# Reordering the score products and computing each token's values once in a banded-attention and mixture-of-experts kernel

## The chip, the cores and the metric

The kernel runs on one core of a Trainium2 chip. The metric is the device time of one execution in microseconds (us). Three executions of the kernel before the change took 786.92, 786.96 and 787.59 us; the median is 786.96 us. One more execution was recorded by the hardware profiler and gave the trace that all views below are read from.

## What is computed

Input x holds 16 sequences (batches) of 512 tokens with 128 features. Cut to what matters, the reference is:

```python
mod = (silu(c) @ wmod).reshape(16, 6, 1, 128)        # sa, ca, ga, sb, cb, gb per batch
h = layernorm(x) * (1 + ca) + sa
q, k, v = h @ wq.T + bq, h @ wk.T + bk, h @ wv.T + bv    # 16 heads of 8 features
scores = q k^T * 8**-0.5, only where |i - j| <= 32       # window of 32 tokens either way
x = x + ga * (softmax(scores) @ v) @ wo.T + bo ...
h = layernorm(x) * (1 + cb) + sb
gate = softmax(h @ gate_w.T); top 2 of 8 experts per token
x = x + gb * (sum of the 2 routed experts + one shared expert)   # silu(h@w1) * (h@w3) @ w2
```

## The kernel before, in words

**Tiles.** A batch is four blocks of 128 tokens. Attention works on one block at a time: a *step* is (batch b, block u), 64 steps in all. Because keys lie up to 32 tokens outside a block, `hT` (normalized input, features on partitions) and `kT` are padded by 32 zero columns on either side.

**One step** (the loop in lines 1026 to 1050) issues, in this order:

1. `weights` (line 424): score products into two PSUM tiles `t` of two banks each, with the negated row maximum added by a matmul; then `exp(0)` on ScalarE (line 444, `w<-t`) for the first tile.
2. `average` (line 449): for the step before, 64 small matmuls of `w` with `v_own`, the values; they go into spare columns of a score tile `s`. ScalarE copies the sums out as `raw` (line 464).
3. `transposed` (line 415): four matmuls `neg` turn the next step's row maxima, and ScalarE copies them as `sh` (line 421). Then `other_half`, which is `exp(1)`.
4. `between(b, u, 0)`: a place. A place runs closures from the table `places` (lines 950 to 969), then routing and scattering work.
5. `divided` (line 998): two transposes of `raw` (line 471), then `rec` and `o` on VectorE (lines 474 and 475), which end the softmax.
6. `between(b, u, 1)`, where most steps start a *gated product*: two products `uv` into a PSUM tile, tanh on ScalarE (`g`, line 554), two VectorE operations (`g` and `h`, lines 555 and 557). It is `uv_sh`, `g_sh`, `h_sh` (shared expert, batch b-2) in a batch's first step, and a group of routed rows in the other three once routed rows exist.
7. `look_ahead(n + 3)`: `row_max` (line 386) of the step three ahead: 4 band matmuls and 32 score matmuls into two PSUM tiles `s`, then two VectorE maxima `neg` (line 402), then GpSimd splits them into bf16 pieces (lines 408 to 412).
8. `between(b, u, 2)` and `between(b, u, 3)`: other transposes and products. In a batch's first step these are `oT` (line 497) and `ys` (line 535, the shared expert's last product, which reads `h_sh`); in the second `xT` and `xnT`; in the third `xT`, `h2T`, `q`, `lg`; in the fourth `xT` and `k`.

The order of all engines' instructions is this written order (`manual_schedule`); each engine runs its own list in order and waits for semaphores.

**Buffers that decide waits.** PSUM pool `ps_s` has three tiles of two banks (tag `s`), shared by `t`, `s` and the gated products. Pool `ps_m` has two one-bank tiles (tag `m`, function `misc`) that serve every transpose and every other product in turn, so each waits for the reader of the one two before it. `average` writes into the second `s` tile of the last `row_max`, taken from the list `spare`.

**Values.** `project_v` (line 358) computes a batch's values for eight overlapping windows of 128 keys, one every 64 tokens: 8 matmuls, in two halves of 4, each half in one PSUM tile followed by one ScalarE copy (line 369) into one of three `v_own` tiles. It runs in places (1, 0) and (3, 0) of the batch before. A `v_own` tile keeps a head's 8 values, a column of ones and zeros up to 32 columns.

Of the kernel before, what the change touches and what calls it, by code (L numbers as in the profile page):

```python
# [10 lines left out]
F32 = mybir.dt.float32  # L11
# [8 lines left out]
P = 128  # L20
B, S, D = 16, 512, 128
H, DH, WINDOW = 16, 8, 32
E = 8
NT = S // P
QB = 64
# [4 lines left out]
NU = S // U  # L30
G, J = 4, 4
SP = S + 2 * WINDOW
# [18 lines left out]
def adaln_block(ctx: ExitStack, tc: tile.TileContext, x, wq, bq, wk, bk, wv, bv, wo, bo,  # L51
# [3 lines left out]
    const = ctx.enter_context(tc.tile_pool(name="const", bufs=1))  # L55
# [5 lines left out]
    def mm(o, lhsT, rhs, start=True, stop=True):  # L61
        nc.tensor.matmul(o, lhsT, rhs, start=start, stop=stop)  # L62
# [81 lines left out]
    pieces_of = [const.tile([P, 4, G, 32], BF16, name=f"pieces{n}") for n in range(NPC)]  # L144


    NVO = 3
    v_own_of = [const.tile([P, 2, 4 * 8 * 32 + 16], F32, name=f"v_own{n}") for n in range(NVO)]
    smallT = const.tile([P, 27], F32, name="smallT")
    modT = const.tile([P, 6, B], F32, name="modT")  # L150
    wT = [const.tile([P, D], F32, name=f"wT{n}") for n in range(4)]
    wqT, wkT, wvT, woT = wT
# [22 lines left out]
    with ExitStack() as c1:  # L175
# [5 lines left out]
        def misc(name):  # L181
            return ps_m.tile([P, 512], F32, tag="m", name=name)
# [65 lines left out]
        def zero_but_ones(t):  # L248
            nc.gpsimd.memset(t, 0.0)
            nc.gpsimd.memset(  # L250
                t[:, :, 0 : 4 * 8 * 32].rearrange("p s (m c) -> p s m c", c=32)[:, :, :, DH : DH + 1], 1.0
            )

        def operands():
# [5 lines left out]
        def more_operands():  # L260
            for t in pieces_of[2:]:
                nc.gpsimd.tensor_copy(t.rearrange("p i g r -> p (i g r)"), pieces_0)
            zero_but_ones(v_own_of[2])
            nc.gpsimd.memset(zero, 0.0)

        def gate(t, shape, name):
# [90 lines left out]

        def project_v(b):

            m = made[b]  # L360
            hT = m.hT
            m.v_own = []
            for half in range(2):
                ps = misc(f"v_{b}_{half}")
                for n in range(4):
                    i = half * 4 + n
                    mm(ps[:, n * D : (n + 1) * D], hT[:, i * QB : i * QB + P], wvT)
                t = v_own_of[(2 * b + half) % NVO]
                nc.scalar.copy(
                    t[:, :, 0 : 4 * 8 * 32].rearrange("p s (m c) -> p m s c", c=32)[:, :, :, 0:DH],  # L370
                    ps.rearrange("p (m s c) -> p m s c", s=2, c=DH),
                )
                m.v_own += [(t.rearrange("p s c -> p (s c)"), 8 * n) for n in range(4)]
                yield

        def edge(u):
# [72 lines left out]
        def average(b, u, w, v_own):  # L449

            t = spare.pop() if spare else ps_s.tile([P, 2, 512], F32, tag="s", name=f"o_{b}_{u}")
            spare.clear()
            w = w.rearrange("p g (a h j q) -> p g a h j q", a=2, h=2, j=J)
            for a in range(2):
                c = slice(4 * KM + a * QB, 4 * KM + (a + 1) * QB)
                v, m0 = v_own[2 * u + a]
                for s in range(2):
                    for n in range(2):
                        for g in range(G):
                            k0 = s * 4 * 8 * 32 + (m0 + 2 * g + n) * 32  # L460
                            mm(t[32 * g : 32 * g + 32, n, c], v[:, k0 : k0 + 32], w[:, g, a, :, 2 * n + s, :],
                               start=s == 0, stop=s == 1)
            raw = wk_p.tile([P, 2, U], F32, tag="raw", name=f"raw_{b}_{u}", bufs=2)
            nc.scalar.copy(raw, t[:, :, 4 * KM : 4 * KM + U])
            return raw
# [445 lines left out]
        def routing():  # L911

            for g, r in list(routes.items()):
                if next(r, 0) is None and g < len(GROUPS):
                    return

        def scattering():
            if scatters and next(scatters[0], 0) is not None:
                scatters.pop(0)
                n_sorted[0] += 1  # L920

        raw_of = []
        AHEAD = 3
# [4 lines left out]
        def projecting(b):  # L928
            if b < B:
                if b not in projects:  # L930
                    projects[b] = project(b)
                    values[b] = project_v(b)
                next(projects[b], None)
# [42 lines left out]
        def between(b, u, n):  # L976
            for f in places.get((u, n), []):
                f(b)
            if n < 3 or b == B - 1:
                routing()  # L980
            if n == 0 and raw_of:
                window[:] = [None, raw_of[-1]]
                scattering()
                combining()
                window.clear()
            n_places[0] += 1
            fetch_some()

        def look_ahead(n):
            if n < len(steps):  # L990
                b, u = steps[n]
                maxima[b, u] = row_max(b, u, made[b].kT, made[b].q_own)
# [11 lines left out]
        with tc.manual_schedule():  # L1004
            nc.gpsimd.memset(neg_half, -0.5)
            projecting(0)
            before_first()
            operands()
            for _ in range(5):
                projecting(0)  # L1010
            look_ahead(0)
            projecting(1)
            projecting_v(0)
            projecting_v(0)
            look_ahead(1)
            projecting(1)
            more_operands()
            transposed(0)
            projecting(1)
            look_ahead(2)  # L1020
            projecting(1)
            once = before_second()
            copies = experts_and_zeros()
            spare.clear()
            pending = None
            for n, (b, u) in enumerate(steps):
                m = made[b]
                if u == 0:
                    m.o = act.tile([P, NT, D], F32, tag="o", name=f"o_{b}")
                w, other_half = weights(b, u, m.kT, m.q_own, maxima.pop((b, u)))  # L1030
                if pending is not None:
                    raw = average(*pending)
                    raw_of[:] = [raw]
                transposed(n + 1)
                other_half()
                between(b, u, 0)
                if pending is not None:
                    divided(pending, raw)
                if n == 0:
                    projecting(1)  # L1040
                between(b, u, 1)
                if n == 0:
                    projecting(1)
                look_ahead(n + AHEAD)
                between(b, u, 2)
                if n < 3:
                    next(once, None)
                next(copies, None)
                between(b, u, 3)
                pending = (b, u, w, m.v_own)  # L1050

            beat_c()
            beat_b()
            divided(pending, average(*pending))
            for n in range(2):
                load_every(n)
            units = [(b, e) for b in range(SORTED, B) for e in (E, *range(E))]
            t = ps_s.tile([P, 2, 512], F32, tag="s", name="sums")
            sums += [t[:, n, :] for n in range(2)]
            x_next = h_last = None  # L1060
            stores = []

            def tick():
                for b in range(B - 3, B):
                    finishing(b)
                routing()
                window[:] = [None, None]
                scattering()
                combining()
                window.clear()  # L1070
                n_places[0] += 2
                fetch_some()

            while units or x_next or h_last or stores or len(stream) > n_done[0] or combines:
                tick()
                beat_a()
                stores = [r for r in stores if next(r, 0) is None]
                x_now, x_next = x_next, None
                if units and units[0][0] in h2T_of and (units[0][1] == E or units[0][0] in scores_T):
                    x_next = (*units[0], scaled(*units.pop(0)))  # L1080
                beat_b()
                h_now = None
                if x_now:
                    b, e, xe = x_now
                    h_now = b, e, gated(f"all_{b}_{e}", lambda o, n: mm(o, matrices(e)[n], xe), 0, 1)
                tick()
                beat_c()
                if h_last:
                    added(*h_last)
                    if h_last[1] == E - 1:  # L1090
                        stores.append(stored(h_last[0]))
                h_last = h_now
            assert n_done[0] == len(stream) and not combines
# [81 lines left out]
```

## Time and profile before

| what | value |
|---|---|
| median of three executions | 786.96 us |
| profiled execution, its own time | 860.98 us |
| its span, first to last instruction | 859.2 us |
| mean granted TensorE clock | 0.931 |
| TensorE busy (page, part 1) | 80% of the span |
| VectorE, ScalarE, GpSimd busy | 52%, 49%, 50% |
| 64 steps: first `t` to the start of the last step | 30.2 to 674.9 us |
| the tail: routed rows of the last batches, two batches computed by all experts | 674.9 to 859.2 us |

A reader of the page takes part 1 (busy time by engine) first, then part 4 (the chain of work that ended last). The trace also gives groups of instructions by form (busy time, mean ns of one, idle time before them and what ended it), a list of waits (who waited for whom: total us, times, longest), and a timeline in which each row has the start, the length, the engine, the line, and what it writes and reads. In those, PE is TensorE, PEld its weight loads, DVE VectorE, ACT ScalarE, POOL GpSimd. The profiled execution is 74 us longer than the median of the others.

### The profile page before, as it was taken

The page shows a single profiled execution, that of the slowest core. Times are in us where ns is not written, and L with a number is a line of the kernel's source. Part 1 is how long each engine was busy: PE and PEld are TensorE (multiplying, and loading weights), DVE is VectorE, ACT ScalarE, POOL GpSimd, SP SyncE. Part 2 cuts the span into 40 slices and gives each one's busy share as a digit, 9 for nine tenths or more (in the row PEclk, how much of TensorE's full clock was granted, in tenths as well). Part 3 has the DMA queues.
Part 4 walks back from the last instruction along what each step waited for, and adds up shares of the span by engine and source line. Part 5 has one row for each costly group of instructions (what it writes and reads, how often), then busy time and mean ns, then how long its engine had stood idle before and what let it go on. Part 6 is the DMA issues. An engine that isn't in the chain of part 4 may idle for free.

```text
span 859.2 us, 26167 instructions
## 1 busy us (share of the span) xinstructions
PE 687.0 (80%) x10792; PEld 513.3 (60%) x10792; DVE 443.9 (52%) x1058; ACT 423.2 (49%) x733; POOL 426.0 (50%) x934
## 2 busy tenths in 40 slices
PE   5889999877898888987888897789868564866980
PEld 3557677655676766676766676566656453544630
DVE  2544656835358354445655254763637433654482
ACT  3657777555675554654555555546433421222310
POOL 3533333486522566526466564555553646334265
PEclk9999999999999998998899999999988777998896
DMA  5071301112332435361453345345314344666644
GB/s 168 3 217 40 92 7 39 41 33 69 102 105 74 122 98 161 87 171 29 134 176 106 115 119 158 100 130 150 113 54 137 111 150 125 199 200 202 185 108 109
DMA packets 119510, 97.49 MB, mean 113 GB/s; under 512 B 9125, under 2 KB 113487, under 8 KB 119391
## 3 DMA queue, kind: packets, MB, share of 16 engines
q1 hardware_dynamic: 91834, 70.70, 29.3%
q0 software_dynamic: 7168, 14.69, 5.7%
q10 hardware_dynamic: 20388, 10.43, 4.1%
q8 instruction: 84, 1.38, 0.7%
q14 instruction: 36, 0.29, 0.1%
HBM read 66.39 MB, written 30.97 MB: 113 GB/s over the span
## 4 chain that ended last, share of the span: by engine, by line
PE 48%; DVE 13%; issue 13%; ACT 10%; POOL 6%; another core or an unknown queue 5%; DMA 3%; SPq 2%; POOLq 0%; DVEq 0%; ACTq 0%
PE s L62 12%; PE t L62 9%; PE uv L62 5%; POOL yg L806 4%; DVE neg L402 3%; ACT w L444 2%; PE q L62 2%; PE uv_sh L62 2%; PE xT L211 2%; PE raw L471 2%; PE ys L62 2%; PE ye L62 2%; PE lg L62 2%; PE v L62 2%
## 5 line engine op out<-in xcount | busy, mean ns | idle before, releaser
L444 ACT ACTIVATE w<-t 128x1024 f32<-128x1024 f32 x128 | 131.6, 1028 | 70.3 <-PE t L62 62.9
L806 POOL DMA_INDIRECT yg<-result,r_posi x112 | 110.7, 989 | 92.8 <-DVE yg L819 45.4
L402 DVE TENSOR_REDUCE neg<-s 128x8 f32<-128x768 f32 x128 | 116.8, 953 | 55.2 <-PE s L62 21.9
L410 POOL CAST pieces<-neg 128x16 bf16<-128x16 f32 x192 | 56.2, 293 | 163.8 <-DVE neg L402 154.2
L724 POOL DMA_INDIRECT table<-rows,r_posi x112 | 112.1, 1001 | 26.2 <-issue 25.5
L62 PEld LDWEIGHTS s<-w,v_own 128*32 128x32 f32 x3904 | 64.0, 115 | 42.0 <-issue 27.1
L62 PE MATMUL s<-w,v_own 128*32 128x64 f32 x3904 | 78.5, 228 | 9.7 <-issue 9.4
L62 PE MATMUL uv<-xT,wg 128*128 128x128 f32 x608 | 82.1, 293 | 0.2 <-issue 0.2
L62 PEld LDWEIGHTS <-packed 32*128 32x128 bf16 (+2 forms) x1101 | 32.4, 95 | 83.0 <-issue 68.4
L62 PEld LDWEIGHTS uv<-xT,wg 128*128 128x128 f32 x608 | 77.8, 207 | 6.1 <-issue 5.7
L62 PE MATMUL t<-q_own,kT 32*128 32x256 f32 x1024 | 77.5, 411 | 0.0
L62 PE MATMUL s<-kT,q_own 32*128 32x96 f32 x2048 | 71.9, 274 | 3.0 <-issue 2.0
L474 DVE RECIPROCAL rec<-raw 128x16 f32<-128x16 f32 x64 | 16.2, 253 | 111.7 <-PE raw L471 111.7
L62 PEld LDWEIGHTS s<-kT,q_own 32*128 32x128 f32 x2048 | 70.9, 193 | 3.7 <-issue 3.6
L555 DVE SCALAR_TENSOR_TENSOR g<-g,uv 128x512 f32<-128x512 f32 x38 | 26.1, 687 | 73.2 <-issue 33.2
L62 PE MATMUL t<-packed 32*128 32x256 bf16 x512 | 35.1, 289 | 26.7 <-DVE neg L402 20.6
L62 PEld LDWEIGHTS t<-q_own,kT 32*128 32x128 f32 x1024 | 54.0, 205 | 2.8
L774 ACT COPY xT<-xT 128x512 f32<-128x512 f32 x38 | 22.2, 585 | 67.6 <-PE xT L211 43.2
L554 ACT ACTIVATE g<-uv 128x512 f32<-128x512 f32 x38 | 22.7, 598 | 62.2 <-PE uv L62 29.7
L211 PE MATMUL xT<-wide,xg 128*128 128x128 f32 x152 | 28.3, 302 | 27.5 <-DMA xg<-table 14.6
L195 POOL TENSOR_SCALAR veps_f<-mv_f 128x4 f32<-128x4 f32 x16 | 5.7, 356 | 77.0 <-DVE mv_f L191 77.0
L62 PE MATMUL ye<-wg,h 128*128 128x128 f32 x304 | 42.6, 284 | 0.2 <-DVE xe L843 0.2
(188 smaller groups left out, 1340.9 us busy)
## 6 DMA issues: line engine op xcount, KB each, us to landing
wg<-experts SPq DMA_DIRECT2D x152, 192.0 KB
xg<-table SPq DMA_DIRECT2D x38, 256.0 KB
result<-ye ACTq DMA_DIRECT2D x38, 256.0 KB
mb<-mod_rows SPq DMA_DIRECT2D x16, 320.0 KB
x<-in_L_attn_x_dram SPq DMA_DIRECT2D x16, 256.0 KB
table<-zero SPq DMA_DIRECT2D x8, 512.0 KB
out_dram<-x SPq DMA_DIRECT2D x16, 256.0 KB
xb<-out_dram SPq DMA_DIRECT2D x14, 256.0 KB
```

The lines of the kernel that those rows point to most:

```text
L62: nc.tensor.matmul(o, lhsT, rhs, start=start, stop=stop)
L211: nc.tensor.transpose(ps[:, t * P : (t + 1) * P], src[:, t, :], ident)
L402: nc.vector.tensor_reduce(neg[:, :, 2 * n : 2 * n + 2].rearrange("p i g -> p g i"), tiles[n][:, :, 0 : 4 * KM].rearrange("p g (i k) -> p g ...
L410: nc.gpsimd.tensor_copy(pieces[:, :, :, n], neg)
L444: nc.scalar.activation(w[:, 2 * n : 2 * n + 2, :], tiles[n], AF.Exp, scale=SCALE)
L471: nc.tensor.transpose(ps[:, n * P : (n + 1) * P], raw[:, n, :], ident)
L474: nc.vector.reciprocal(rec, both[:, :, DH])
L554: nc.scalar.activation(a, t[:, 0, :], AF.Tanh, scale=0.5)
L555: nc.vector.scalar_tensor_tensor(a, a, 1.0, t[:, 0, :], ALU.add, ALU.mult)
L724: stored = nc.gpsimd.indirect_dma_start(out=table[g % 2][:, :], out_offset=bass.IndirectOffsetOnAxis(ap=r.pos[:, k, n0 + t : n0 + t + 1], ...
L774: nc.scalar.copy(xT, ps)
L806: nc.gpsimd.indirect_dma_start(out=y[:, t, :], out_offset=None, in_=result[g][:, :], in_offset=bass.IndirectOffsetOnAxis(ap=r.pos[:, k, s ...
```

## The change

It makes two edits.

**Order within a step.** `look_ahead(n + 3)` moves from behind `between(b, u, 1)` to directly behind `between(b, u, 0)`, ahead of `divided`. So the `s` matmuls and the two `neg` maxima now come before the `raw` transposes, before `rec` and `o`, and before the step's gated product. (In the very first step two pieces of `project(1)` move along with it.)

```diff
                 between(b, u, 0)
+                if n == 0:
+                    projecting(1)
+                    projecting(1)
+                look_ahead(n + AHEAD)
                 if pending is not None:
                     divided(pending, raw)
-                if n == 0:
-                    projecting(1)
                 between(b, u, 1)
-                if n == 0:
-                    projecting(1)
-                look_ahead(n + AHEAD)
                 between(b, u, 2)
```

**Values once per token.** `project_v` computes the 576 padded tokens once, in 4 matmuls of 128 rows and one of 64, and copies them to two tiles, `even` (windows that begin at a multiple of 128) and `odd` (those that begin 64 later). The odd tile's halves come from different partitions, so there are six ScalarE copies instead of two. There are four `v_own` tiles, 48 columns for a pair of heads instead of 64.

```diff
-    NVO = 3
-    v_own_of = [const.tile([P, 2, 4 * 8 * 32 + 16], F32, name=f"v_own{n}") for n in range(NVO)]
+    PAIR = 48
+    v_own_of = [const.tile([P, 4 * 8 * PAIR], F32, name=f"v_own{n}") for n in range(4)]
...
-            for half in range(2):
-                ps = misc(f"v_{b}_{half}")
-                for n in range(4):
-                    i = half * 4 + n
-                    mm(ps[:, n * D : (n + 1) * D], hT[:, i * QB : i * QB + P], wvT)
...
+            for k0, k1 in ((0, 3), (3, 5)):
+                ps = misc(f"v_{b}_{k0}")
+                for k in range(k0, k1):
+                    r = min(P, SP - k * P)
+                    mm(ps[0:r, (k - k0) * D : (k - k0 + 1) * D], hT[:, k * P : k * P + r], wvT)
+                last = min(k1, NT)
+                put(even, 0, k0, ps, 0, slice(0, last - k0), P)
+                put(odd, 0, k0, ps, QB, slice(0, last - k0), QB)
+                first = max(k0, 1)
+                put(odd, QB, first - 1, ps, 0, slice(first - k0, k1 - k0), QB)
                 yield
...
-                            k0 = s * 4 * 8 * 32 + (m0 + 2 * g + n) * 32
+                            k0 = (m0 + 2 * g + n) * PAIR + s * 16
```

`put` is one ScalarE copy of `rows` partitions from PSUM to a `v_own` tile. The first half has 3 matmuls and copies of 128x384, 64x384 and 64x256; the second has 2 matmuls and copies of 128x128, 64x128 and 64x256. `average` still issues 64 matmuls of the same shapes per step. At the start, four tiles of 128x1536 are zeroed on GpSimd instead of three of 128x2080.

More of the change, by code (lines that the diff above doesn't have):

```diff
@@ L250, in zero_but_ones @@
             nc.gpsimd.memset(
-                t[:, :, 0 : 4 * 8 * 32].rearrange("p s (m c) -> p s m c", c=32)[:, :, :, DH : DH + 1], 1.0
+                t.rearrange("p (m k c) -> p m k c", k=3, c=16)[:, :, 0:3:2, DH : DH + 1], 1.0
             )
@@ L262, in more_operands @@
                 nc.gpsimd.tensor_copy(t.rearrange("p i g r -> p (i g r)"), pieces_0)
-            zero_but_ones(v_own_of[2])
+            for t in v_own_of[2:]:
+                zero_but_ones(t)
             nc.gpsimd.memset(zero, 0.0)
@@ L361, in project_v, with put @@
             hT = m.hT
-            m.v_own = []
-            for half in range(2):
-                ps = misc(f"v_{b}_{half}")
-                for n in range(4):
-                    i = half * 4 + n
-                    mm(ps[:, n * D : (n + 1) * D], hT[:, i * QB : i * QB + P], wvT)
-                t = v_own_of[(2 * b + half) % NVO]
+            even, odd = (v_own_of[(2 * b + n) % 4] for n in range(2))
+            m.v_own = [((even, odd)[i % 2], 8 * (i // 2)) for i in range(2 * NU)]
+            def put(t, p0, k, ps, p1, n, rows):
+                m0, m1 = 8 * k, 8 * (k + n.stop - n.start)
                 nc.scalar.copy(
-                    t[:, :, 0 : 4 * 8 * 32].rearrange("p s (m c) -> p m s c", c=32)[:, :, :, 0:DH],
-                    ps.rearrange("p (m s c) -> p m s c", s=2, c=DH),
-                )
-                m.v_own += [(t.rearrange("p s c -> p (s c)"), 8 * n) for n in range(4)]
+                    t[p0 : p0 + rows].rearrange("p (m k c) -> p m k c", k=3, c=16)[:, m0:m1, 0:3:2, 0:DH],
+                    ps[p1 : p1 + rows, n.start * D : n.stop * D].rearrange("p (m s c) -> p m s c", s=2, c=DH),
+                )
+            for k0, k1 in ((0, 3), (3, 5)):
[8 more added lines that the diff above has]
+                put(odd, QB, first - 1, ps, 0, slice(first - k0, k1 - k0), QB)
                 yield
```

## The prediction

> **What bounds it now.** I read the page first, part 1 and part 4:
>
> ```profile
> PE 687.0 (80%) x10792; PEld 513.3 (60%) x10792; DVE 443.9 (52%) x1058; ACT 423.2 (49%) x733; POOL 426.0 (50%) x934
> PE 48%; DVE 13%; issue 13%; ACT 10%; POOL 6%; another core or an unknown queue 5%; DMA 3%; SPq 2%; POOLq 0%; DVEq 0%; ACTq 0%
> ```
>
> TensorE (PE) is the fullest engine and carries half of the chain; a quarter of the chain is VectorE and ScalarE, work that TensorE stands waiting for. So a change here pays or costs in two ways: by TensorE's own work, and by what lies between a product and the product that needs its result. The list of waits says which results come last:
>
> ```profile
> PE t L62 <- DVE neg L402: 20.6, 19, 3.7
> PE raw L471 <- ACT raw L464: 15.2, 22, 5.0
> PE ys L62 <- DVE h_sh L557: 3.8, 7, 0.7
> ```
>
> The first two are what the new order addresses. The third is small only because of what stands ahead of `ys`. That shows in the timeline of batch 8's first step (its `t` begins at 304.90):
>
> ```profile
> 307.73 0.37 ACT L464 COPY raw<-s 128x256 f32<-128x256 f32 x1
> 308.15 0.44 PE L471 MATMUL raw<-wide,raw 128*128 128x128 f32 x2 [0.40 <-ACT raw L464]
> 308.42 1.88 PE L62 MATMUL uv_sh<-h2T,ws_sb 128*128 128x512 f32 x4
> 308.46 1.05 ACT L444 ACTIVATE w<-t 128x1024 f32<-128x1024 f32 x1
> 310.24 0.34 PE L62 MATMUL s<-packed 32*128 32x384 bf16 x4
> 310.34 0.60 ACT L554 ACTIVATE g_sh<-uv_sh 128x512 f32<-128x512 f32 x1 [0.83 <-PE uv_sh L62]
> 310.41 1.03 PE L62 MATMUL s<-kT,q_own 32*128 32x96 f32 x32
> 310.97 0.69 DVE L555 SCALAR_TENSOR_TENSOR g_sh<-g_sh,uv_sh 128x512 f32<-128x512 f32 x1 [1.76 <-ACT g_sh L554]
> 311.37 0.66 PE L211 MATMUL oT<-wide,o 128*128 128x128 f32 x4
> 311.69 0.69 DVE L557 SCALAR_TENSOR_TENSOR h_sh<-g_sh,uv_sh 128x512 f32<-128x512 f32 x1
> 312.52 1.13 PE L62 MATMUL ys<-ws_sb,h_sh 128*128 128x128 f32 x8 [0.49 <-issue]
> ```
>
> `uv_sh` ends at 310.3; tanh and two VectorE operations take until 312.4. Of these 2.2 us TensorE fills 1.14 with `s` and 0.65 with `oT`; it idles 0.49. The change takes `s` out of this gap.
>
> **Reordering, a batch's first step.** Batches 2 to 15 have `uv_sh` here. In the new order `s` follows `neg`. It does not run free: of its two PSUM tiles, the second is the one that `average` wrote into, so as built its third matmul waits for the copy `raw` (308.10), as the `raw` transposes did. Only two band matmuls (some 0.1 us) slip ahead. Then: `s` ends 309.3, `raw` 309.65, and `uv_sh`, whose PSUM tile is now the one that `exp(1)` empties (309.51), starts at 309.6 instead of 308.42. `ys` follows `uv_sh`'s start by 4.1 us as before, since tanh, `g_sh` and `h_sh` are unchanged: 313.7 instead of 312.5, **+1.16**. Eight batches (2, 3, 5, 6, 8, 9, 11, 12) are of this kind: +9.3.
>
> In batches 4, 7 and 10 routing fills VectorE, as in batch 7:
>
> ```profile
> 264.21 0.17 DVE L652 CAST r_cntb<-r_cnt 128x8 bf16<-128x8 f32 x1
> 264.30 0.25 DVE L474 RECIPROCAL rec<-raw 128x16 f32<-128x16 f32 x1
> 264.58 0.29 DVE L475 TENSOR_TENSOR o<-raw,rec 128x128 f32<-128x128 f32 x1
> 264.79 0.68 DVE L555 SCALAR_TENSOR_TENSOR g_sh<-g_sh,uv_sh 128x512 f32<-128x512 f32 x1
> 265.50 0.69 DVE L557 SCALAR_TENSOR_TENSOR h_sh<-g_sh,uv_sh 128x512 f32<-128x512 f32 x1
> 266.11 1.82 DVE L402 TENSOR_REDUCE neg<-s 128x8 f32<-128x768 f32 x2
> ```
>
> VectorE is back to back, and `ys` waits for `h_sh`. The new order puts the 1.82 us of `neg` ahead of `rec`: +1.85 with the gap between instructions, 3 times, +5.6. Behind `neg` now stand `rec`, `o`, `g`, `h`, and `oT` and `ys` wait for those. The Trainium skill, TensorE: Matmul & The Clock Gate, section Architectural detail, speaks against the change here: ScalarE's and VectorE's queues are strict FIFO. Taken alone it would charge 1.85 in all 14 first steps, 26 us; but in batch 8 VectorE idles 1.76 before `g_sh`, and `neg` fits into that hole. The rows decide: 1.85 only where they are back to back. Batches 13 to 15 have a second gated product or other waits there: between 0 and 1.9 in one, I take +1 together. Batch 1's first step has no `uv_sh`; `oT`'s fourth transpose then waits for `o`, which stands behind `neg`: +1.1. Sum: **+17.0**.
>
> **Reordering, the other steps.** With routed rows (`uv`), `t`'s second tile waited for `neg` behind `h`; as built it waits for `h`, and `neg` is done long before. Measured from the end of `uv` in batch 8's second step: before, 2.1 to the end of `h` and 0.95 for the first `neg`, 3.05; after, `uv` ends 1.2 later and `h` follows 2.1 behind, 3.3. So the 20.6 us wait is renamed, +0.25 per step, where `xT` and `xnT` (1.2) or `xT` and `k` (1.5) do not cover it; in the third steps they, `q` and `lg` do. Where VectorE is back to back in second steps (batches 7, 10, 13: routing positions), `h` ends one `neg` later: +1.0 each, +3.0. Without routed rows (second steps of batches 1 to 6) nothing stands between, and the earlier `neg` clears TensorE's stall of 0.5 there; third steps of these, -0.1 each: together -0.5x6-0.6 = -3.6. The wait for `raw` is passed to `s`, saved at nothing.
>
> **Values.** These rows, grouped by form:
>
> ```profile
> L62 PE MATMUL v<-wT,hT 128*128 128x128 f32 x256 | 36.7, 286 | 3.4 <-ACT ye L789 1.9 <-DVE x L505 0.9 <-issue 0.6
> L369 ACT COPY v_own<-v 128x512 f32<-128x512 f32 x32 | 18.9, 590 | 20.2 <-PE v L62 17.2 <-ACT ye L789 2.7 <-POOL pieces L410 0.3
> L464 ACT COPY raw<-s 128x256 f32<-128x256 f32 x61 | 22.5, 369 | 19.4 <-PE s L62 9.1 <-remote 9.0
> ```
>
> 256 records are 128 matmuls, 36.7/128 = 0.287 us each. 48 go: -13.8 us of TensorE work, of which 16 fall in second steps (-0.29 per batch) and 32 in fourth (-0.58). The trace has no 64-row product; it costs between half and all of 0.287, I take all. ScalarE: 590 at 512 columns and 369 at 256 give 0.86 ns a column and 150 ns fixed, so the first half's three copies cost 479+479+369 = 1.33 and the second's 259+259+369 = 0.89, against 0.59 each; +1.04 a batch, 16.6 us. The 64-partition copies have no row: between half and all of a full copy's, I take all. The Trainium skill, ScalarE: Activation LUTs, section What ACT_TABLE_LOAD costs, gives 186 ns + 0.833 ns a column, less 93 ns where instructions follow each other: an estimate of 2.0 against 1.2 a batch, +0.8. It speaks against six copies too; I keep the rows. What covers them is ScalarE's idle time: after `v` in second steps `s`, `raw` and `uv` keep TensorE busy 3.4 us before the next tanh. If that cover were gone, 16.6 would be on the path. It is gone once: in fourth steps without `uv` (batches 1 to 5) `k`, whose PSUM tile is the one that `v` filled, waits for the copies; those five steps lose the 0.58 gained and 0.15 more, +0.75 in all.
>
> In second steps the -0.29 pays where TensorE is late (batches 1 to 6: -0.2 more each beyond the stall cleared, -1.2) and cancels the +0.25 in batches 8, 9, 11, 12, 14. In fourth steps with `uv` (batches 6 to 14) `raw` no longer waits 0.25 for the copy `ye`; -0.58-0.25+0.25 = -0.55 with overlaps, 9 times: -5.0. Zeroing on GpSimd: one tile took 1.84; 4x1536 against 3x2080 columns is -0.1 us, hidden at the start by the waits for weights, between -0.5 and +1; taken as 0. Issue of DMAs moves in no queue.
>
> **Sum** for the profiled execution (860.98): 17.0 + 3.0 - 3.6 + 0.75 - 1.2 - 5.0 = **+11 us**. The median of the timed runs is 0.914 of that execution; scaled, +10.0. Predicted: **797 us**, slower by 1.3%. By the unknown copies, products and first steps of batches 13 to 15 it lies between 791 and 803.
>
> **Rivals.** *The maxima escape a stall (0.2).* TensorE lost 2.45, 2.5, 2.23 and 3.69 us at the first steps of batches 5, 6, 13 and 15 and 0.6 to 0.9 at four others, some 13.8 us, because `neg` started 1 to 2.8 us late while GpSimd ran four indirect DMAs in a row. An earlier `neg` may run ahead of these. For it: `rec` and `o` before it started on time. Against it: `g` and `h` would then stand in the same window. It decides when over 10 of the 13.8 are saved; at all of it, 11-13.8 = -2.8, 784 us, no slower than before; at most of it 788.
> *The saved products pay in full (0.06).* If waits for `h_sh` are shorter without a profile, 13.8 us of products are left: 771 to 783.
> *VectorE's queue binds everywhere (0.12).* If `h` is late by a whole `neg` in more steps than the seven counted, 10 more steps cost 10 to 18: 804 to 812.
> The case above has 0.62. *The copies hide nothing* is inside the last.
>
> **Numbers.** 0.2% (1.6 us) is about what a measurement can tell from no change. Slower: 0.62+0.12+0.04 = 0.78; same: 0.09 of the first rival; faster: 0.07+0.06 = 0.13. The range takes the likeliest case and the first rival, 785 to 804.
>
> **What would show it.** In the profile after: 160 records of `v` and 96 copies `v_own`; `ys <- h_sh` growing from 3.8 to about 20 us; `t <- neg` nearly gone, `t <- h` in its place; a new wait of `s` for the copy `raw`; in batch 8's first step `ys` some 8.8 us behind the first `t` instead of 7.6. If `ys` does not wait longer, the sum is wrong in its largest term; if starts of `neg` late by over 1 us are gone, the first rival is right.

## The result, and the profile after

The changed kernel takes 819.88 us (median of four, 813.45 to 828.56) against 786.94 for the one before: ratio 1.0396, 95% interval 1.0322 to 1.0471. Timed a second time (e5 below) the ratio was 1.0461 (1.0396 to 1.0527). A ratio here is taken from the fast executions of both kernels, with its own 95% interval, so it need not equal the quotient of the medians beside it. The prediction, 797 with a range of 785 to 804, had the direction and missed the size: +33 to +37 us instead of +10.

The profiled execution of before that the prediction was read from (860.98 us) cannot be laid beside the changed kernel's (817.38 us): it shows stalls of its own, those of e0 below. A later profile of the kernel before, e4, ran in 794.41 us, near its timed runs. All comparisons below are with e4. Parts 1 and 4 of its page:

```profile
PE 668.7 (84%) x10792; PEld 504.8 (64%) x10792; DVE 442.4 (56%) x1058; ACT 425.5 (54%) x733; POOL 425.5 (54%) x934
PE 40%; DVE 21%; issue 13%; POOL 12%; ACT 10%; DMA 3%; POOLq 0%; DVEq 0%; ACTq 0%; SPq 0%
```

and of the changed kernel's:

```profile
PE 662.3 (81%) x10696; PEld 496.1 (61%) x10696; DVE 443.6 (54%) x1058; ACT 441.6 (54%) x797; POOL 419.3 (51%) x936
PE 44%; DVE 21%; POOL 11%; ACT 8%; issue 8%; DMA 7%; SPq 1%; POOLq 0%; DVEq 0%; ACTq 0%
```

TensorE is busy for 6 us less and the span is 23 us longer (815.6 against 792.6): it stands still more. Part 4 does not say for whom: VectorE has 21% of the chain in both. The 23 us are fewer than the 33 between the medians, because e4's execution was 5.4 us above the median of its chip (788.99) and this one 2.5 under its own. Who TensorE stands still for is in the lists of waits (us in total, times, longest; only the rows that matter here). Before, e4:

```profile
PE t L62 <- DVE neg L402: 14.1, 24, 2.8
PE ys L62 <- DVE h_sh L557: 6.2, 11, 0.9
PE oT L211 <- DVE o L475: 5.1, 4, 4.1
PE t L62 <- DVE h L557: 3.0, 6, 0.6
```

After:

```profile
PE t L62 <- DVE h L569: 13.0, 16, 2.4
PE ys L62 <- DVE h_sh L569: 13.0, 10, 1.7
PE oT L212 <- DVE o L487: 12.8, 6, 4.6
PE t L62 <- DVE neg L414: 6.2, 4, 2.6
...
PE h2T L212 <- DVE o L487: 5.0, 3, 2.1
```

`ys` waits twice as long for `h_sh`, and `t <- neg` turned into `t <- h`, both as forecast. Not forecast is `o`: the waits for it, `oT`, `h2T`, `xnT` (4.4), `q` (4.0) and `lg` (2.7) together, are 28.9 us, against 10.4 in e4 (`oT` 5.1, `xnT` 2.8, `q` 2.5).

Two steps show the two mechanisms. In batch 8's first step (its `t` begins at 306.27) `ys` starts 9.42 us behind `t`, where e4 has 7.90. First e4's `ys`, then the changed kernel (here and below, rows of other work are left out):

```profile
301.01 0.66 PE L211 MATMUL oT<-wide,o 128*128 128x128 f32 x4
302.16 1.13 PE L62 MATMUL ys<-ws_sb,h_sh 128*128 128x128 f32 x8 [0.50 <-DVE h_sh L557]
```

```profile
311.32 1.82 DVE L414 TENSOR_REDUCE neg<-s 128x8 f32<-128x768 f32 x2 [2.15 <-PE s L62]
311.48 1.98 PE L62 MATMUL uv_sh<-h2T,ws_sb 128*128 128x512 f32 x4
313.30 0.71 PE L212 MATMUL oT<-wide,o 128*128 128x128 f32 x4
...
314.13 0.69 DVE L567 SCALAR_TENSOR_TENSOR g_sh<-g_sh,uv_sh 128x512 f32<-128x512 f32 x1 [0.50 <-ACT g_sh L566]
...
315.69 1.13 PE L62 MATMUL ys<-ws_sb,h_sh 128*128 128x128 f32 x8 [1.67 <-DVE h_sh L569]
```

Behind `uv_sh` only `oT` is left to do, and TensorE idles 1.67 us; VectorE is free before `g_sh` (0.50), so its queue is not at fault here. In the same batch's third step it is. Again e4 first:

```profile
320.46 0.29 DVE L475 TENSOR_TENSOR o<-raw,rec 128x128 f32<-128x128 f32 x1
321.69 0.60 PE L211 MATMUL h2T<-wide,h 128*128 128x128 f32 x4
322.12 1.81 DVE L402 TENSOR_REDUCE neg<-s 128x8 f32<-128x768 f32 x2
```

```profile
334.12 1.82 DVE L414 TENSOR_REDUCE neg<-s 128x8 f32<-128x768 f32 x2
335.85 0.25 DVE L486 RECIPROCAL rec<-raw 128x16 f32<-128x16 f32 x1
336.13 0.29 DVE L487 TENSOR_TENSOR o<-raw,rec 128x128 f32<-128x128 f32 x1
...
336.57 0.63 PE L212 MATMUL h2T<-wide,h 128*128 128x128 f32 x4 [1.03 <-DVE o L487]
```

In the changed kernel VectorE runs back to back, `neg` stands ahead of `rec` and `o`, and `h2T` waits for `o`. `h2T` does not read `o`: it takes the `ps_m` buffer that `raw` had, and `o` is the last reader of `raw`.

From the first `t` to the start of the last step ("the loop"), by kind of step, worked out from the trace rows:

| | e4 (before) | changed kernel | e5 (changed, again) |
|---|---|---|---|
| profiled execution's own time | 794.41 | 817.38 | 828.45 |
| loop | 595.0 | 616.4 | 626.8 |
| first steps of all batches | 151.2 | 171.6 | 170.8 |
| second steps | 145.3 | 144.3 | 149.6 |
| third steps | 174.0 | 180.3 | 188.2 |
| fourth steps | 124.4 | 120.2 | 118.1 |
| TensorE idle in the loop | 65.8 | 91.0 | 94.3 |
| half of TensorE's busy time at half clock | 24.9 | 22.0 | 30.9 |
| loop less that half | 570.1 | 594.4 | 595.9 |
| third steps less their share of it | 158.9 | 172.2 | 175.3 |

The loop holds 21.4 of 23.0 us and 31.8 of 34.0; TensorE's idle time grew by 25.2 and 28.5. The 10.4 us between the two executions of the one kernel are TensorE's clock for the most part: e5 ran 70.6 us of its loop at half clock, the other 50.2. Half of TensorE's busy time in such stretches is an estimate of what they cost. Less that estimate the two executions agree to 1.5 us, and the change costs the loop 24.3 and 25.8 us.

### The profile page after: what moved, and what is told of

It reads as the page before. It is cut to its first block, busy times and chain, and to the rows that moved or that the text cites. A ratio compares the mean times of both kernels' runs of the same rounds, so it can differ in the third digit from the quotient of the medians.

```text
span 815.6 us, 26075 instructions
## 1 busy us (share of the span) xinstructions
PE 662.3 (81%) x10696; PEld 496.1 (61%) x10696; DVE 443.6 (54%) x1058; ACT 441.6 (54%) x797; POOL 419.3 (51%) x936
## 3 DMA queue, kind: packets, MB, share of 16 engines
q1 hardware_dynamic: 91834, 70.70, 30.2%
## 4 chain that ended last, share of the span: by engine, by line
PE 44%; DVE 21%; POOL 11%; ACT 8%; issue 8%; DMA 7%; SPq 1%; POOLq 0%; DVEq 0%; ACTq 0%
PE s L62 11%; PE t L62 8%; DVE neg L414 5%; PE uv L62 5%; POOL yg L818 4%; PE ye L62 3%; DMA yg<-result,r_posi 3%; POOL table L736 2%; PE ys L62 2%; PE q L62 2%; PE uv_sh L62 2%; PE lg L62 2%; DMA table<-rows,r_posi 2%; ACT w L456 2%; PE y L62 2%
## 5 line engine op out<-in xcount | busy, mean ns | idle before, releaser
L422 POOL CAST pieces<-neg 128x16 bf16<-128x16 f32 x192 | 51.0, 266 | 101.0 <-DVE neg L414 92.6
L62 PEld LDWEIGHTS uv<-xT,wg 128*128 128x128 f32 x608 | 76.0, 203 | 6.7 <-issue 3.6
L62 PEld LDWEIGHTS s<-w,v_own 128*32 128x32 f32 x3904 | 61.0, 115 | 28.1 <-issue 22.2
L62 PE MATMUL t<-q_own,kT 32*128 32x256 f32 x1024 | 75.6, 406 | 0.0
L62 PE MATMUL s<-w,v_own 128*32 128x64 f32 x3904 | 71.1, 228 | 0.0
L62 PEld LDWEIGHTS s<-kT,q_own 32*128 32x128 f32 x2048 | 66.8, 188 | 1.4 <-issue 1.4
L62 PE MATMUL t<-packed 32*128 32x256 bf16 x512 | 33.4, 287 | 19.2 <-DVE h L569 13.0
L371 ACT COPY v_own<-v 128x384 f32<-128x384 f32 (+2 forms) x96 | 35.5, 370 | 15.2 <-PE v L62 11.2
L721 DVE TENSOR_TENSOR rows<-h,r_top 128x512 f32<-128x512 f32 x28 | 20.3, 725 | 42.7 <-DMA table<-rows,r_posi 42.7
L62 PEld LDWEIGHTS ye<-wg,h 128*128 128x128 f32 x304 | 39.0, 197 | 5.8 <-issue 5.5
```

What stands on the lines that cost most here:

```text
L371: nc.scalar.copy(t[p0 : p0 + rows].rearrange("p (m k c) -> p m k c", k=3, c=16)[:, m0:m1, 0:3:2, 0:DH], ps[p1 : p1 + rows, n.start * D : n ...
L422: nc.gpsimd.tensor_copy(pieces[:, :, :, n], neg)
L721: nc.vector.tensor_tensor(rows, h2_of[b], r.top[:, k, n0 : n0 + NT].unsqueeze(2).to_broadcast([P, NT, D]), ALU.mult)
```

## The experiments

Two theories for the loss: **A**, TensorE's order: the score products no longer fill its wait for tanh, `g` and `h`. **B**, VectorE's order: `neg` ahead of `rec` and `o` delays what needs `o` or its buffer. A third, **C**, blames the values' copies. Kernels listed together ran on one chip; "early" means the scores in the changed kernel's place.

**e0 to e3, on one chip (before: 877.77 us).** e0 is the kernel before, unchanged.

> The kernel before, unchanged, with a new profile. The profiled execution of before took 860.98 us, 74 us more than its own timed runs. If the waits were priced from a disturbed execution, the new profile is near 787 us, the entries for 'another core or an unknown queue' are gone, the starts of neg that came late by over 1 us shrink, and the loop from the first t to the start of the last step takes some 590 us instead of 645. If the profiled execution stood for all, the new one is near 860 again.

It took 881.77 us, and here the timed runs are as slow. Neither alternative holds as it was put. The profiled execution of 860.98 us was no freak: it has the late starts described next and a tail of 184.3 us (e0: 186.3), so it looks like one from such a chip. Batch 7's third step in e0:

```profile
291.70 0.96 POOL L724 DMA_INDIRECT table<-rows,r_posi  x1 [0.21 <-issue]
293.71 1.82 DVE L402 TENSOR_REDUCE neg<-s 128x8 f32<-128x768 f32 x2 [2.50 <-remote]
293.83 0.59 ACT L774 COPY xT<-xT 128x512 f32<-128x512 f32 x1 [4.05 <-remote]
```

and in e4:

```profile
282.34 1.82 DVE L402 TENSOR_REDUCE neg<-s 128x8 f32<-128x768 f32 x2
282.57 0.96 POOL L724 DMA_INDIRECT table<-rows,r_posi  x1 [0.22 <-issue]
```

In e0 the scores end at 290.3, `xT` at 290.9; VectorE and ScalarE start 1 us after the fourth of GpSimd's indirect DMAs has ended. In e4 `neg` starts ahead of that DMA, as soon as VectorE is free. Counting starts of `neg` over 1 us behind both its scores and VectorE's previous instruction: 16 with 30.2 us in the trace that the prediction was read from, 16 with 32.9 us in e0, none in e4 nor in the changed kernel's two traces.

e1 is the values alone:

```diff
-                look_ahead(n + AHEAD)
                 if pending is not None:
                     divided(pending, raw)
                 between(b, u, 1)
+                look_ahead(n + AHEAD)
```

> Values once per token, in the old order. The order is the cause (main theory): the values save TensorE work in second and fourth steps, 5 to 8 us by the prediction's own terms, so 779 to 785 us. The rival, that the six ScalarE copies and the four v_own tiles stand on the path: 795 us or more, most of the 33 us that the change cost.

876.58 us, ratio 0.9965 (0.9938 to 0.9991): a small gain on this chip, not the 5 to 8 us, and no sign of C here (e8 has one).

e2 is the order alone (the old `project_v` in the changed loop).

> The new order, with values as before. If the order is the cause: 820 to 828 us, that is the whole cost of the change and what the values saved. If the values' copies are the cause: 797 us or less (the order's +10 to +15 by the prediction's sum). If the two only cost together: both single edits stay under 800.

940.19 us, 1.0719 (1.0651 to 1.0786). The order is the cause, and costs more here than the whole change did on its chip: late starts of `neg` are 58.1 us in e2 against 32.9 in e0, 18 of them, each beside a run of GpSimd's indirect DMAs, with `rec` and `o` behind `neg` in the queue.

e3 puts the maxima behind `rec` and `o` (`row_max` is split into products and maxima):

```diff
-                look_ahead(n + AHEAD)
+                look_ahead(n + AHEAD, later=True)    # score matmuls only
                 if pending is not None:
                     divided(pending, raw)
+                look_end(n + AHEAD)                  # the two maxima, the pieces
```

> The change, with the score matmuls in the new place but the two VectorE maxima (and GpSimd's pieces) issued behind rec and o instead of ahead of them. Theory A, the score matmuls no longer fill TensorE's wait between uv and h: nothing comes back, 816 to 822 us, and ys waits for h_sh as long as in the change. Theory B, neg stands ahead of rec and o in VectorE's queue, and o empties the PSUM buffer that oT, xnT, h2T and q wait for: the waits for o (some 30 us with all four) go, 795 to 805 us. Half and half would be 806 to 814.

935.85 us, 1.0665 (1.0597 to 1.0733): nothing to speak of came back. The expected times were given for a chip of 787 us; by ratio the answer is A's, but this run cannot decide. No `neg` starts late in its trace; now `rec`, which stands ahead of it, does: over 1 us behind both the `raw` transposes and VectorE's previous instruction 21 times, 71.2 us in all. By steps the loss moved: third and fourth steps take 207.6 and 139.1 us against 217.1 and 157.9 in e2, first steps 225.1 against 195.7.

**e4 to e7, on one chip (before: 788.99 us).** e4 is the kernel before, e5 the changed one, both unchanged.

> The kernel before, unchanged, for a profile beside the next three. In two profiled executions so far (860.98 and 881.77 us) VectorE's maxima neg started up to 4.8 us late while GpSimd issued indirect DMAs; in the changed kernel's profile (817.38 us) none did. If that lateness belongs to the chip and not to the kernel, this execution is either near 787 us without late starts of neg and with a tail (last step's start to the end) of some 170 us, or near 870 us with them and a tail of 185 us; nothing between.

> The changed kernel, unchanged. If this chip shows the late starts: ratio to before of 1.065 to 1.07 (order alone gave 1.072, values alone 0.9965 there); if not, 1.04 as in the first comparison.

794.41 us for e4, with no late start and a tail of 168.7 us (e0: 186.3): the lateness belongs to the chip. e5: 826.42 us, as expected without it.

e6 leaves VectorE in the old order and TensorE in the new one:

```diff
                 between(b, u, 1)
+                look_end(n + AHEAD)
```

> The change, with the score matmuls in the new place, but the two VectorE maxima and GpSimd's pieces behind the step's gated product, where they were before. TensorE's order is the changed kernel's, VectorE's the old one. Theory A (the score matmuls no longer fill TensorE's wait behind uv): nothing comes back, ratio as the change's within 0.007. Theory B (neg stands ahead of rec, o, g and h in VectorE's queue): at least two thirds of the loss comes back, ratio under 1.02.

822.78 us, 1.0461 (1.0410 to 1.0513): the changed kernel's ratio. Its third steps are back at 172.9 us (e4: 174.0), as B says, but its first steps stay at 169.3, and `t` now waits for `neg` 21.9 us and for `h` 16.2. (The profiled execution, 811.55 us, is the lowest of its six.) B's part is real. Giving it back alone buys nothing clear (medians of 822.78 and, in e5, 826.42): the maxima are then late for `t`. Less the half-clock estimate its loop is 594.8 us, the changed kernel's; third steps are at 158.0 (e4: 158.9), second steps 5.2 us longer.

e7 has early scores in first steps only:

```diff
-                look_ahead(n + AHEAD)
+                if u == 0:
+                    look_ahead(n + AHEAD)
                 if pending is not None:
                     divided(pending, raw)
                 between(b, u, 1)
+                if u != 0:
+                    look_ahead(n + AHEAD)
```

> The change, but with the scores early only in a batch's first step (where uv_sh, oT and ys stand behind them); in the other three steps they are where they were. The prediction put +17 of its +11 us there and let the other steps win. If that split is right: slower than the whole change, ratio 1.015 to 1.04. If the other steps carry the loss (waits of h2T, xnT, q and k for o): ratio 1.00 to 1.02, under half of the change's loss.

815.78 us, 1.0346 (1.0278 to 1.0414). First steps carry most of the loss.

**e8 to e11, on one chip (before: 790.18 us).** e8 is e1's kernel again.

> Values once per token in the old order, measured more closely. By the changed kernel's rows the products save 0.54 us a batch (1.16 to 0.93 and 1.07 to 0.76), 8.6 us in all, of which some 5 lie in the fourth steps. If they pay there: ratio 0.990 to 0.997. If the six copies take it back: 1.00 or more.

794.81 us, 1.0056 (1.0027 to 1.0084): slower by half a percent. The gain expected in e1 did not come, and the second alternative here did: on this chip the values have a small cost of their own, C's part. Batch 8's fourth step shows why the saved products do not pay, e4 first, then e8:

```profile
329.32 0.44 PE L471 MATMUL raw<-wide,raw 128*128 128x128 f32 x2 [0.25 <-ACT ye L789]
```

```profile
329.42 0.44 PE L483 MATMUL raw<-wide,raw 128*128 128x128 f32 x2 [0.56 <-ACT ye L801]
```

The products `v` took 1.07 us in e4 and 0.76 in e8 there; the 0.31 us saved is waited for: `raw` starts 4.94 us into the step in both, when the copy `ye` empties its buffer. And the first steps of batches 3 and 6 begin `raw` 0.26 us later (3.50 instead of 3.24), because ScalarE, with four more copies a batch, is later with the copy `raw`.

e9 gives the cover back and leaves `o` late:

```diff
-                look_ahead(n + AHEAD)
-                if pending is not None:
-                    divided(pending, raw)
                 between(b, u, 1)
+                look_ahead(n + AHEAD)
+                if pending is not None:
+                    divided(pending, raw)
```

> The change, but with the step's gated product (uv or uv_sh) issued ahead of the scores, and the raw transposes, rec and o still behind them. The scores again fill TensorE's wait for tanh, g and h; rec and o stay behind neg. Theory A (what costs is the lost cover behind uv): ratio 0.99 to 1.01, ys waits for h_sh some 7 us in all as in the old order. Theory B (what costs is the late o): ratio 1.03 or more, and the waits for o stay near 30 us.

875.80 us, 1.1041 (1.0974 to 1.1108), far more than either theory said. The waits are B's alone, one row of them 45.5 us:

```profile
PE oT L212 <- DVE o L487: 45.5, 16, 8.2
```

In batch 8's first step VectorE runs `g_sh`, `h_sh`, `neg`, and only then `rec` and `o`. Timeline rows, and then the window behind the wait from the table by windows (start and end, length, busy time of PE, PEld, DVE, ACT, POOL, granted clock, DMA share, GB/s):

```profile
338.16 0.48 PE L212 MATMUL oT<-wide,o 128*128 128x128 f32 x1 [2.52 <-DVE o L487]
338.43 1.92 PE L62 MATMUL ys<-ws_sb,h_sh 128*128 128x128 f32 x8
```

```profile
338.60:343.00 4.40, 4.40 (x93) 3.57 (x95) 1.38 (x2) 2.81 (x6) 1.96 (x6) 0.68 0.11 34
```

The wait of 2.52 us is followed by a second loss: the granted clock falls to half for 3.41 us (from 337.98), and `ys` takes 1.92 us instead of 1.13. Over the loop e9 is 81.9 us longer than e4: 48.0 us idle, and 33.8 more busy, with 144.4 us at half clock against 57.4.

e10 moves `divided` ahead of the early scores; `uv` stays behind them.

```diff
-                look_ahead(n + AHEAD)
                 if pending is not None:
                     divided(pending, raw)
+                look_ahead(n + AHEAD)
                 between(b, u, 1)
```

> The change, but with the raw transposes, rec and o ahead of the scores; the gated product stays behind the scores. Theory A: as the change, ratio 1.035 to 1.05, ys waits for h_sh as long. Theory B: the waits for o fall to some 10 us as in the old order and two thirds of the loss comes back, ratio under 1.02.

817.24 us, 1.0361 (1.0307 to 1.0416), A's expectation. Third steps are back at 175.0 us, but less the half-clock estimate they are at 165.6, halfway between e4 (158.9) and the changed kernel (172.2): the late `o` is about half of their loss. The wait for `o` in them is at e4's level (2.6 us against 2.5; changed kernel 11.6), while `t` waits for VectorE's `neg` and `h` 17.5 us against e4's 13.6; `neg` still stands ahead of `g` and `h` here, and not in e6. The first steps stay at 173.0, since `o` is free but the cover is not:

```profile
PE ys L62 <- DVE h_sh L569: 19.4, 10, 2.4
```

e11 is the reverse of e7, with the two conditions exchanged.

> The change, but with the old order in a batch's first step and the scores early in the other three. The reverse edit (early only in the first step) gave 1.0346. If the steps add up: 1.005 to 1.015. If first steps alone carry the loss: 0.99 to 1.00. The prediction's own terms for these steps and the values make -6 us, 0.992.

801.71 us, 1.0122 (1.0080 to 1.0163): the steps add up. Both e7 and e11 contain the values (+0.56%), so 3.46 + 1.22 - 0.56 = 4.1%, between the two measurements of the whole change. By steps e11 stands to e4: second -1.8, third +10.1, fourth -4.5 us.

**e12 to e15, on one chip (before: 873.30 us).** These have e7's edit with other conditions: early scores in second and fourth steps (e12, `u in (1, 3)`), in the fourth alone (e13, `u == 3`), e12's order with the old `project_v` (e14); e15 is e2's kernel again.

> The change, but with the scores early only in a batch's second and fourth steps. By the steps of the runs so far (early in all but the first, against before: second steps -1.8 us, third +10.1, fourth -4.5) the loss of the other three steps is the third step's alone; without it: 0.991 to 0.998, faster than before. If early scores cost in the following step instead: 1.00 to 1.01.

> The change, but with the scores early only in a batch's fourth step, where the copy ye keeps the raw transposes waiting and the scores can fill that wait: the saved products should pay there, 0.6 us in each of eight steps, against values alone. Values alone 1.0056, so 0.997 to 1.002; if the fill is worth nothing, 1.004 to 1.008.

> As the first of these, with values as before. If the values need the new order to pay in fourth steps, this is slower than the first by 2 to 6 us (ratio 0.997 to 1.004); if their copies cost more than their products save even there, it is faster than the first.

> The new order in all steps with values as before, on the kind of chip where the change costs 4 to 4.6%. If values cost 0.5% here whatever the order, 1.035 to 1.041; if they pay once the order is new, 1.045 to 1.055.

Ratios 1.0213 (1.0170 to 1.0256), 1.0129 (1.0087 to 1.0170), 1.0227 (1.0182 to 1.0271), 1.0570 (1.0491 to 1.0648). This was the kind of chip with late starts (20 of them, 43.6 us, in e12), and all expectations, made for the other kind, missed. e12 and e14 overlap: the values make no difference there that can be told. e15 and e2 are one kernel, and their intervals do not overlap (1.0570 against 1.0719), so the two chips with late starts are not alike either.

**e16 and e17, on one chip (before: 788.96 us)**: e12's and e2's kernels.

> Scores early only in second and fourth steps, values once per token, once more. On the kind of chip where before takes some 873 to 878 us it gave 1.0213. If VectorE's late starts there (while GpSimd issues indirect DMAs) are what made it lose, a chip without them (before at some 787 us) gives 0.991 to 1.002; if the order itself loses in these steps, 1.01 or more on either kind.

> The order alone once more. On a chip without late starts: 1.035 to 1.041 if the values cost some 0.5% in the changed kernel too, 1.045 to 1.055 if they pay once the order is new. On the other kind of chip: 1.055 to 1.075 as before.

e16: 788.34 us, 0.9978 (0.9956 to 1.0000). Without late starts (none in its trace) it is level with the kernel before or 0.2% ahead; with them it lost 2.1%. It is the best form of the change found and no clear gain. e17: 819.74 us, 1.0380 (1.0340 to 1.0419): the order alone makes the whole loss. Beside 1.0396 and 1.0461 for the changed kernel, what the values do in it is between nothing and +0.8%.

## Why the prediction was wrong, point by point

| term of the sum | predicted | changed kernel less e4 | e5 less e4 |
|---|---|---|---|
| first steps | +17.0 | +20.4 | +19.6 |
| second steps (+3.0 - 3.0 - 1.2) | -1.2 | -1.0 | +4.3 |
| third steps | -0.6 | +6.3 | +14.2 |
| fourth steps (-5.0 + 0.75) | -4.25 | -4.2 | -6.3 |
| start and tail | 0 | +1.6 | +2.2 |

Less the half-clock estimate the two columns become +18.6 and +18.1 in first steps, -2.7 and -3.4 in second, +13.3 and +16.4 in third, -4.9 and -5.3 in fourth. So measured, the third steps are nearly the whole miss.

- **First steps: mechanism right, size a little short.** "+1.16" in eight of them was 1.27 or 1.28 in batches 2, 3, 5 and 6, and 1.51 or 1.52 in 8, 9, 11 and 12: 11.1 instead of 9.3. In the routing batches 4, 7 and 10 they gave 3.3, 1.1 and 0.6, 5.1 instead of 5.6. Batch 1 gave 1.8 instead of 1.1, and batches 13 to 15, taken at +1, gave 2.5, all of it in batch 15. In the eight, removing the late `o` (e10) leaves the loss standing, so it is the cover, as argued. `uv_sh` also starts where the working put it, behind `exp(1)`: that ends at 311.43 in batch 8, `uv_sh` starts at 311.48. The new wait of `s` for the copy `raw` did not show; its listed waits are for `w`, 5.2 us. A wait for `ys` "to about 20 us" was too much: 13.0, for part of the delay lies in the later start of `uv_sh`.
- **The step that failed: "in the third steps they, `q` and `lg` do"** (cover the wait). The working followed VectorE's queue only to `h` and asked whether `t` would be covered. It did not ask who waits for `o`, except at batch 1's `oT` and in routing steps. `o` empties the `raw` buffer, which `h2T` or `xnT` takes two uses later; with `neg` ahead of it, it is later by up to the 1.82 us of the maxima where VectorE is busy. That turned -0.6 into +6.3 and +14.2 (+13.3 and +16.4 without the clock). e6, with VectorE's old order and TensorE's new one, gives all of it back in these steps, so `neg`'s place in VectorE's queue is shown to be the cause. e10, with `rec` and `o` alone ahead of `neg`, gives back about half, so `o` is that half. The other half was not isolated; e10's longer wait of `t` points to `g` and `h` behind `neg`. Part may come from the neighbouring steps: e16, with its third steps in the old order, has 163.3 in them, 4.4 above e4. The rule of strict order in a queue, weighed against the rows, held in the first steps; it bit in steps where it was not looked for.
- **Fourth steps and the values.** -4.25 was hit by luck: the reason given, saved products, holds only in part. With the old values (e17) fourth steps are at 119.5 us, -4.9, and the values alone leave the step in the fence of e8 at the same length. It is the early `s` that fills `raw`'s wait for `ye`. As an edit by itself the values were credited with a gain; e8 shows a cost of 0.56%.
- **The copies' price was right**: 96 copies, 35.5 us in all or 2.22 a batch, against 1.33 + 0.89 from the rows; the second estimate, 2.0, from a figure that its page gives for ACTIVATE, was short for these copies. Taking all for 64 rows or partitions was right too: a copy of 64x384 takes 476 ns, of 128x384 481; the 64-row product 298 ns, the full ones 290.
- **Rival 1 fell for a reason outside the kernel**: the 13.8 us of stalls by late `neg` exist only on one kind of chip. There the new order makes late starts worse (58.1 against 32.9 us). Rival 3, "VectorE's queue binds everywhere", was nearest, but with `h` as what is late; it was `o` for about half of the third steps' loss, and its range of 804 to 812 was too low as well.
- **The base.** Scaling by 0.914 treated the profiled execution as a stretched copy of the timed ones. It differed in kind, with its own stalls. Here that cost little: 1 us of the sum.

The direction was right because the first steps outweigh the rest. Of the 23 and 34 us, 11 were foreseen; the third steps add 6.9 and 14.8, the first 3.4 and 2.6, the second 0.2 and 5.5. Those parts contain TensorE's clock, which differs from one execution to the next; the estimate without it leaves 24.3 and 25.8 us for the loop. What stays open is what beside `o` is late in the third steps.

## What to carry to other kernels

When a long instruction moves forward in a strict queue, list everything now behind it and follow each to the end of its buffers: not only who reads the result, but who takes the PSUM tile that its last reader frees. Before moving a product out of a gap, ask what else fills the gap; here the scores were the only filler behind `uv_sh`. And a saved instruction ahead of a wait for somebody else saves nothing.

## What the runs showed of the hardware that was not expected

- **Two kinds of chip.** The kernel before takes 785 to 796 us on three of the chips used and in the first measurement, and 865 to 886 on two. On the latter its tail is longer as well (186.3 against 168.7 us) and VectorE and ScalarE start up to 4.9 us late around GpSimd's indirect DMAs. The trace names "remote" as the releaser; what holds them up was not found. One and the same kernel loses 2% there (e12, 1.0213) and nothing elsewhere (e16, 0.9978).
- **Half clock behind short waits.** The granted clock is 1.0 or 0.5, and stretches at half clock in the loop last 3.41 us or a multiple of it. In e9 there are eight waits of 2.52 us in first steps, and a half-clock stretch begins between 0.7 us before the end of the wait and 0.9 us after it in all eight. Shorter waits do it at times: in the changed kernel's trace none begins behind the 1.67 us wait that ends at 315.69 (batch 8), but one does 1.4 us behind the wait of the same length that ends at 235.89. So the length of one wait does not decide alone. The Trainium skill, TensorE: Matmul & The Clock Gate, section HAM oscillation — how this bites in real kernels, gives the rule as no idle gaps over about 3.4 us; in e9's trace 2.52 us were followed by half clock each time.
